# The last half row of a linear-kernel attention in two query parts, its last 256 tokens closed tile against tile

## The chip, the cores and the metric

The kernel runs on one core of one Trainium2 chip. The core has five engines that run side by side, each through its own list of instructions in order: TensorE (PE, matrix multiplication; PEld are its weight loads), VectorE (DVE), ScalarE (ACT), GpSimd (POOL) and SyncE (SP, which here only issues DMAs). They wait for one another through semaphores. The metric is the device time of one launch in microseconds; the median of several runs counts.

## What is computed

Four blocks follow one another on an input of 4 rows of 1024 tokens, 256 features each (4096 tokens). The third block is the one that the change touches, and the fourth begins where it ends:

```python
x = x + _layernorm(_L0_attn_ref(_layernorm(x), ...))      # gated attention
x = x + _layernorm(_L0_ffn_ref(_layernorm(x), ...))       # low-rank feed-forward
x = x + _layernorm(_L1_attn_ref(_layernorm(x), ...))      # the block of the change
x = x + _layernorm(_L1_ffn_ref(_layernorm(x), ...))       # experts, each with its 1024 best tokens

def _L1_attn_ref(x, w_qkv, w_out, b_out, gamma, beta):    # 16 heads of 16 features
    def kernel_func(q, k):
        scores = jnp.einsum('bhqd,bhkd->bhqk', q, k) / jnp.sqrt(HD)
        w = jax.nn.relu(scores)
        return w / (jnp.sum(w, axis=-1, keepdims=True) + KERN_EPS)
    ...
    out = jnp.einsum('bhqk,bhkd->bhqd', kernel_func(q, k), v)
    y = x + out @ w_out + b_out
    return layernorm(y) * gamma + beta

def _L1_ffn_ref(x, Wg, W1, b1, W2, b2):
    S = sigmoid(x @ Wg).T                                  # 8 experts x 4096 tokens
    G, I = jax.lax.top_k(S, 1024)
    ...
```

The weights of the attention are a plain `relu` of the scores; the sum that divides them comes out of the same matmul as the values, as a 17th column of ones.

## The kernel before

**Tiling of the attention.** Tokens come in tiles of 128; a half row is 512 tokens (`TB`, four tiles, `NJ = 4`), and there are eight half rows, `t` = 0 to 7. For the 512 queries of a half row the loop runs over four head groups `g` (four heads at a time) and within each over the eight key tiles `kt` of the row: 32 steps. `g` splits into `t, r = divmod(g, 2)`: two groups, `r` = 0 and 1, fill one half `t` of the 256 features.

**One step.** `scores` (L1225) gives four matmuls of 32 rows each, one head per 32-row strip of TensorE, side by side: 128 keys against 512 queries. Two of them go to single PSUM banks (tag `s`, three banks that the rest of the attention's small matmuls share), two to a pair of banks (tag `d`, two pairs). ScalarE applies `relu` to each single (L1242), VectorE to the pair in one instruction (L1243); the results stand in one of two `w` tiles. `weigh` (L1246) multiplies them with the values, four heads at a time on column strips, and adds over the key tiles into one bank, `po`. The weighing of a step stands behind the scores of the next one, so TensorE's order is scores(i+1), weighing(i).

**End of a head group.** `finish` transposes `po` on VectorE into `turned` (L1281). After `r` = 1 `divide` follows: `by_weight` adds a small constant, inverts and multiplies (L1110 to L1112), `back` transposes into `oT` (L1120).

**Closing a half row.** `close` makes the list of what follows the attention of a half row: `project_out` (eight matmuls `pt` per two tiles, L1135, and the sum `y`, L1142), then, tile by tile for each kind of step: statistics of `y` (`scale_of`: three VectorE instructions, then a power on GpSimd, L1064 to L1067), `affine` (two VectorE instructions, L1155 and L1156), statistics again, `shift` (a small VectorE instruction `msc`, L1160, then ScalarE adds it to `x`, L1162), `add` (L1167), statistics of `x`, and `token_rows` (the normalized token `hg`, L1178, and its DMA to `tok_d`, on SP's queue; after the last tile also `x` to `x_d`). Then `turn_gating` (four transposes per two tiles, `tpg`, L1193, and ScalarE's copy), and `gate` (`pg`, L1207, added to `logits`, L1215).

**The order around it.** The order on TensorE, VectorE and ScalarE is as the program writes it. Two lists hold what is still to do: `beside` (steps with TensorE work) and `rest` (the others). After each step of the attention `go_on` takes one entry of `beside` and one of `rest`, or two of `rest` if `beside` had one; at the last key tile of a group it takes none of `rest`. So the closing of one half row runs beside the attention of the next. The last half row has no next one: after the loop all that is left is emptied, with matmuls of no use (`keep_busy`, L206, which write to an `idle` bank) put in, 8 at first and 63 after the projections.

**After it.** The stage of the experts starts with the sigmoid of `logits` (L1361 to L1364), a search for each expert's threshold in 15 rounds (`ge`, L1394), and the gathering of tokens. SP also brings the experts' biases and weights (L1336 to L1345).

## Time and profile before

| | us |
|---|---|
| median of 3 runs (1630.09 to 1633.78) | 1633.39 |
| the profiled execution, its time | 1633.18 |
| its span | 1631.2 |
| TensorE busy in it | 1569.7 |
| VectorE busy | 920.7 |
| ScalarE busy | 634.7 |
| GpSimd busy | 403.3 |

The page also cuts the span into 40 equal slices of 40.8 us; a digit is the busy share in tenths, and PEclk is the clock granted to TensorE in tenths of full speed:

```profile
PE   7999999999999999999999999983999999999997
DVE  4555566664657787878787888878211211222145
ACT  3344444544544545454545454521121121211233
PEclk9999999999999999999999999995999999999999
```

The attention of the change is the stretch of 7s and 8s of VectorE. Its last half row ends in the slice with an 8 for TensorE; the 3 with half a clock behind it is the search for the thresholds.

In all times below, 0 is the start of the span unless another start is named. A line of the timeline or of the chain of waits gives the start, the length, the engine, the line of the kernel, what is written and read, the number of records, and in brackets the idle time ahead of it with what ended it. A matmul of 32-bit numbers leaves two records, one for each of its two passes.

### The profile page before, as it was taken

How to read it: one execution, taken by the hardware profiler on the slowest of the kernel's cores; microseconds unless marked ns; L12 is line 12 of the kernel's file. 1: busy time of each engine (PE TensorE's matmuls, PEld its weight loads, DVE VectorE, ACT ScalarE, POOL GpSimd, SP SyncE). 2: the span in 40 equal slices, each digit the busy share in tenths (PEclk: the TensorE clock that was granted, in tenths of full speed). 3: DMA queues.
4: the chain of work that ended last, by engine and by line, in shares of the span. 5: the costliest groups of instructions: out<-in, count | busy, mean ns of one | idle time of the engine just before them, and what ended most of it. 6: DMA issues, size and time to landing. Idle time of an engine off the chain costs nothing.

```text
span 1631.2 us, 22623 instructions
## 1 busy us (share of the span) xinstructions
PE 1569.7 (96%) x8787; PEld 778.2 (48%) x8787; DVE 920.7 (56%) x2085; ACT 634.7 (39%) x1101; POOL 403.3 (25%) x439
## 2 busy tenths in 40 slices
PE   7999999999999999999999999983999999999997
PEld 3666666666322232222323222231757667566674
DVE  4555566664657787878787888878211211222145
ACT  3344444544544545454545454521121121211233
POOL 4123232222201011111111001010423324324555
PEclk9999999999999999999999999995999999999999
DMA  8300000000000000101010100040133233234355
GB/s 205 120 1 1 1 1 1 0 1 1 1 1 1 23 18 7 34 7 34 1 40 1 39 2 27 14 168 4 53 78 69 66 74 72 66 75 89 65 148 136
DMA packets 70069, 71.15 MB, mean 44 GB/s; under 512 B 23597, under 2 KB 62922, under 8 KB 69834
## 3 DMA queue, kind: packets, MB, share of 16 engines
q1 hardware_dynamic: 56080, 47.01, 9.4%
q0 software_dynamic: 13008, 21.77, 7.4%
q8 instruction: 69, 1.13, 0.3%
q10 hardware_dynamic: 874, 0.93, 0.2%
q14 instruction: 38, 0.31, 0.1%
HBM read 41.74 MB, written 27.95 MB: 43 GB/s over the span
## 4 chain that ended last, share of the span: by engine, by line
PE 92%; DVE 4%; issue 1%; POOL 1%; ACT 1%; DMA 1%; POOLq 0%; SPq 0%; DVEq 0%; ACTq 0%
PE sc L1233 16%; PE po L1249 16%; PE ph L1712 13%; PE py L1735 13%; PE pg L691 4%; PE py L799 4%; PE pv L707 3%; PE ph L855 2%; PE po L771 2%; PE pt L1135 2%; PE pv L380 2%; PE pq L356 2%; PE pq L876 2%; PE po L775 2%; PE pk L356 2%; PE pkv L786 1%
## 5 line engine op out<-in xcount | busy, mean ns | idle before, releaser
L1243 DVE TENSOR_SCALAR w<-sc 128x1024 f32<-128x1024 f32 x256 | 312.7, 1222 | 97.4 <-PE sc L1233 65.1
L1242 ACT ACTIVATE w<-sc 128x512 f32<-128x512 f32 x512 | 278.0, 594 | 229.6 <-PE sc L1233 102.5
L1233 PE MATMUL sc<-qT,kT 32*128 32x512 f32 x2048 | 293.6, 639 | 1.4 <-ACT w L1242 0.8
L1249 PE MATMUL po<-w,vaug 128*17 128x512 f32 x2048 | 274.7, 598 | 1.3 <-DVE turned L1281 0.3
L1735 PE MATMUL py<-w,hid 128*128 128x256 f32 x1024 | 230.1, 380 | 0.0
L1719 ACT ACTIVATE hid<-ph,mb 128x512 f32<-128x512 f32 (+1 forms) x136 | 90.1, 662 | 344.4 <-PE ph L1712 343.3
L1712 PE MATMUL ph<-xT,w 128*128 128x512 f32 (+1 forms) x544 | 222.8, 567 | 0.7 <-DVE xT L1696 0.7
L1735 PEld LDWEIGHTS py<-w,hid 128*128 128x128 f32 x1024 | 191.1, 190 | 32.0 <-issue 7.0
L1233 PEld LDWEIGHTS sc<-qT,kT 32*128 32x128 f32 x2048 | 80.7, 183 | 184.9 <-issue 170.7
L1712 PEld LDWEIGHTS ph<-xT,w 128*128 128x128 f32 x544 | 103.2, 190 | 111.1 <-issue 107.6
L1249 PEld LDWEIGHTS po<-w,vaug 128*17 128x17 f32 x2048 | 35.3, 95 | 200.3 <-issue 171.0
L1754 POOL DMA_INDIRECT acc_d<-y,idx x56 | 88.1, 1573 | 157.0 <-issue 131.8
L1752 DVE TENSOR_TENSOR y<-py,mb 128x256 f32<-128x256 f32 x56 | 23.4, 418 | 142.3 <-PE py L1735 140.3
L1521 POOL DMA_INDIRECT got<-tok_d,idx x64 | 65.8, 1028 | 152.1 <-DVE idx L1511 135.0
L1696 DVE COPY xT<-tp 128x512 f32<-128x512 f32 (+1 forms) x34 | 22.3, 660 | 91.7 <-PE tp L1691 91.7
L1067 POOL TENSOR_TENSOR rsg<-veg,mhalf 128x1 f32<-128x1 f32 x32 | 17.7, 554 | 219.5 <-DVE veg L1066 219.5
L691 PE MATMUL pg<-nT,wh 128*128 128x512 f32 x128 | 61.4, 611 | 1.5 <-ACT nT L630 1.5
L799 PE MATMUL py<-wo,oT 128*128 128x256 f32 x256 | 61.9, 385 | 0.0
L707 PE MATMUL pv<-wh,nT 128*128 128x512 f32 x128 | 59.7, 592 | 0.0
L1511 DVE CAST idx<-parts 128x8 int32<-128x8 f32 x8 | 1.3, 167 | 101.8 <-PE parts L1509 101.8
L799 PEld LDWEIGHTS py<-wo,oT 128*128 128x128 f32 x256 | 47.3, 190 | 17.2 <-issue 9.4
L572 POOL TENSOR_TENSOR x<-x,y 128x1024 f32<-128x1024 f32 x14 | 32.9, 2351 | 73.3 <-ACT y L561 73.3
(277 smaller groups left out, 1927.5 us busy)
## 6 DMA issues: line engine op xcount, KB each, us to landing
w<-in_L_ffn_W_dram SPq DMA_DIRECT2D x16, 1024.0 KB, 5.7
x<-in_L_attn_x_dram SPq DMA_DIRECT2D x8, 512.0 KB, 5.0
acc_d<-logits SPq DMA_DIRECT2D x8, 512.0 KB, 4.2
x_d<-x SPq DMA_DIRECT2D x8, 512.0 KB, 3.0
tok_d<-hg SPq DMA_DIRECT2D x32, 128.0 KB, 1.7
back_w<-acc_d SPq DMA_DIRECT2D x6, 512.0 KB, 7.4
out_dram<-x SPq DMA_DIRECT2D x20, 128.0 KB, 1.7
out_dram<-back_w POOLq DMA_DIRECT2D x4, 512.0 KB
```

The lines of the kernel that those rows point to most:

```text
L691: nc.tensor.matmul(pg, lhsT=wh[:, c, HID + e * P : HID + (e + 1) * P], rhs=d["nT"][:, c, :], start=(c == 0), stop=(c == DC - 1),)
L707: nc.tensor.matmul(pv, lhsT=d["nT"][:, c, i * P : (i + 1) * P], rhs=wh[:, c, 0:HID], start=(c == 0), stop=(c == DC - 1),)
L799: nc.tensor.matmul(py, lhsT=d["oT"][:, e, :], rhs=wo[:, e, :], start=(e == 0), stop=(e == EC - 1))
L1233: nc.tensor.matmul(sc, lhsT=row["kT"][t][rows, r, kt * P : (kt + 1) * P], rhs=row["qT"][rows, t, qh * TB : (qh + 1) * TB], start=True, sto ...
L1242: nc.scalar.activation(w[:, j, :], sc, AF.Relu)
L1243: nc.vector.tensor_scalar(w[:, 2:4, :], pair, 0.0, None, ALU.max)
L1249: nc.tensor.matmul(po[32 * j : 32 * j + HD + 1, :], lhsT=row["v"][:, kt, HQ * t + 2 * j + r, :], rhs=w[:, j, :], start=(kt == 0), stop=(kt ...
L1521: return nc.gpsimd.indirect_dma_start(out=dst, out_offset=None, in_=rows[:, :], in_offset=self.at_chunk(c), bounds_check=NT - 1, oob_is_er ...
L1712: nc.tensor.matmul(ph, lhsT=w1[:, c, f * P : (f + 1) * P], rhs=xT[u][:, c, h * n : (h + 1) * n], start=(c == 0), stop=(c == DC - 1),)
L1719: nc.scalar.activation(hid[:, f, h * n : (h + 1) * n], ph, AF.Gelu, bias=mb1[:, e * FC + f : e * FC + f + 1])
L1735: nc.tensor.matmul(py, lhsT=hid[:, f, i * P : (i + 1) * P], rhs=w2[:, f, :], start=(f == 0), stop=(f == FC - 1),)
L1754: scatter = nc.gpsimd.indirect_dma_start(out=acc_d[:, :], out_offset=lists[e].at_chunk(k), in_=y, in_offset=None, bounds_check=NT - 1, oob ...
```

## The change

Only the last half row (`t` = 7) is treated differently in the attention, by `halves = 2`; everywhere else `halves` is 1 and the program is as before.

- Its 512 queries are taken in two parts of 256 (`q2` = 0, 1). A step takes two key tiles, so each part has 16 steps; a step has eight score matmuls of 256 columns, and eight weighing matmuls of 256 columns. Both key tiles of a head share a bank. `r` = 0 and 1 use separate halves of `po`.
- In every second step of this half row ScalarE applies `relu` to the pair of banks as well, in one instruction of 1024 columns.
- `go_on` takes two entries of `rest` per step there, four if `beside` had one, and the last key tile of a group is no exception.
- The first part's two tiles are closed through the lists, beside the second part. The second part's two are closed by a new function, `at_once`: each kind of step for one tile, then for the other, with the statistics of both and one power on GpSimd for the two (`moments`). Projection and gate are taken apart into halves; `shift` is not used there (the mean is subtracted from `y` on VectorE instead).
- The filling matmuls are 4 and 34 there, for 8 and 63. In the experts' stage 13 stand for 9.

```diff
+            def moments(tag, src, part):
+
+                st, mv, ve, rs = gating.setdefault(
+                    tag, [wk.tile([P, 2, w], F32, tag=f"{k}z", name=f"{k}{tag}") for k, w in zip(("st", "mv", "ve", "rs"), (6, 2, 1, 1))]
+                )
+                if part == "take":
+                    for k, i in enumerate(tiles):
+                        nc.vector.bn_stats(st[:, k, :], src[:, i, :])
+                    for k in range(2):
+                        nc.vector.bn_aggr(mv[:, k, :], st[:, k, :])
+                    nc.vector.tensor_scalar(ve[:, :, 0], mv[:, :, 1], EPS, None, ALU.add)
+                    nc.gpsimd.tensor_tensor(rs[:, :, 0], ve[:, :, 0], mhalf[:, 0:2], ALU.pow)
+                return [(i, mv[:, k, 0:1], rs[:, k, :]) for k, i in enumerate(tiles)]
+
+            def at_once(by_weight, back):
+
+
+                x, stt = xs[t], nc.vector.scalar_tensor_tensor
+                pts = [(i, side([P, D], "pt")) for i in tiles]
+                for i, pt in pts:
+                    project_tile(pt, i, (0,))
+                idle = ps.tile([P, 2, TB], F32, tag="d", name="idle", bufs=2)[:, 0, :]
+                keep_busy(idle, 4)
+                by_weight()
+                back()
+                for i, pt in pts:
+                    project_tile(pt, i, (1,))
+                keep_busy(idle, 34)
+                for i, pt in pts:
+                    nc.vector.tensor_tensor(y[:, i, :], pt, h[:, i, :], ALU.add)
+                scales = moments("b", y, "take")
+                for i, mean, rs in scales:
+                    stt(y[:, i, :], y[:, i, :], mean, gam, ALU.subtract, ALU.mult)
+                for i, mean, rs in scales:
+                    stt(y[:, i, :], y[:, i, :], rs, bet, ALU.mult, ALU.add)
+                scales = moments("c", y, "take")
+                for i, mean, rs in scales:
+                    nc.vector.tensor_scalar(y[:, i, :], y[:, i, :], mean, None, ALU.subtract)
+                for i, mean, rs in scales:
+                    stt(x[:, i, :], y[:, i, :], rs, x[:, i, :], ALU.mult, ALU.add)
+                for i, mean, rs in moments("g", x, "take"):
+                    token_rows(i, mean, rs)
+                turn_gating(tiles[0])
+                gate()
...
-            for j, sc in enumerate((*singles, pair[:, 0, :], pair[:, 1, :])):
-                rows = slice(32 * j, 32 * (j + 1))
-                nc.tensor.matmul(
-                    sc,
-                    lhsT=row["kT"][t][rows, r, kt * P : (kt + 1) * P],
-                    rhs=row["qT"][rows, t, qh * TB : (qh + 1) * TB],
-                    start=True,
-                    stop=True,
-                )
+            for m in range(halves):
+                for j, sc in enumerate((*singles, pair[:, 0, :], pair[:, 1, :])):
+                    rows = slice(32 * j, 32 * (j + 1))
+                    nc.tensor.matmul(
+                        sc[:, m * n : (m + 1) * n],
+                        lhsT=row["kT"][t][rows, r, (kt + m) * P : (kt + m + 1) * P],
+                        rhs=row["qT"][rows, t, q0 : q0 + n],
+                        start=True,
+                        stop=True,
+                    )
 
             for j, sc in enumerate(singles):
                 nc.scalar.activation(w[:, j, :], sc, AF.Relu)
-            nc.vector.tensor_scalar(w[:, 2:4, :], pair, 0.0, None, ALU.max)
+            if halves > 1 and kt // halves % 2:
+
+                nc.scalar.activation(w[:, 2:4, :], pair, AF.Relu)
+            else:
+                nc.vector.tensor_scalar(w[:, 2:4, :], pair, 0.0, None, ALU.max)
             return w
 
+        def weighed(halves, r):
+
+            return slice(0, TB) if halves == 1 else slice(r * TB // 2, (r + 1) * TB // 2)
...
-                for g in range(NG):
-                    for kt in range(KT):
-                        w = scores(row, qh, g, kt)
-                        if before is not None:
-                            finish(*before)
-
-                        go_on(0 if kt == KT - 1 else 1)
-                        before = (row, b, qh, g, kt, w)
+                halves = 2 if (b, qh) == (B - 1, BPB - 1) else 1
+                for q2 in range(halves):
+                    for g in range(NG):
+                        for kt in range(0, KT, halves):
+                            w = scores(row, qh, q2, halves, g, kt)
+                            if before is not None:
+                                finish(*before)
+
+                            at_end = kt == KT - halves
+                            go_on(halves if halves > 1 or not at_end else 0)
+                            before = (row, b, qh, q2, halves, g, kt, w)
             row = after
         finish(*before)
-        idle = ps.tile([P, 2, TB], F32, tag="d", name="idle", bufs=2)[:, 0, :]
-        keep_busy(idle, 8)
-        while rest and not beside:
-            go_on()
-        while beside:
-            go_on()
-
-        keep_busy(idle, 63)
         while beside or rest:
             go_on()
+        state["close"][0](*divide(state, DC - 1))
...
-            keep_busy(idle, 9)
+            keep_busy(idle, 13)
```

`weigh`, `finish`, `divide`, `close`, `token_rows`, `turn_gating` and `gate` get the same arguments (`halves`, the part's tiles, its columns) and work on them.

## The prediction

> **What bounds the kernel now.** I read the page's costliest groups first, then the windows, then the chain of waits around the end of the attention, then the timeline of the last half row.

> ```profile
> L1243 DVE TENSOR_SCALAR w<-sc 128x1024 f32<-128x1024 f32 x256 | 312.7, 1222 | 97.4 <-PE sc L1233 65.1
> L1242 ACT ACTIVATE w<-sc 128x512 f32<-128x512 f32 x512 | 278.0, 594 | 229.6 <-PE sc L1233 102.5
> L1233 PE MATMUL sc<-qT,kT 32*128 32x512 f32 x2048 | 293.6, 639 | 1.4 <-ACT w L1242 0.8
> L1249 PE MATMUL po<-w,vaug 128*17 128x512 f32 x2048 | 274.7, 598 | 1.3 <-DVE turned L1281 0.3
> ```

> TensorE bounds the attention: its score and weighing groups were idle 1.4 and 1.3 us in 256 steps. A step is 1.07 us of scores and 0.98 us of weighing (starts in the timeline: 1041.04, 1042.12, 1043.10), so 2.05 us. The last half row is 32 steps; its first score starts at 993.82, its last weighing is over at 1069.41, where the filling matmuls start: 75.6 us.

> ```profile
> 993.82:1069.55 75.73, 75.16 (x554) 19.23 (x554) 60.78 (x104) 39.92 (x73) 6.60 (x12) 1.00 0.04 15
> 1069.55:1096.28 26.73, 24.32 (x115) 12.13 (x114) 20.34 (x67) 3.47 (x7) 6.86 (x12) 1.00 0.70 239
> 1100.00:1110.00 10.00, 0.98 (x6) 0.41 (x4) 8.72 (x48) 5.36 (x4) 0.00 (x0) 0.55 0.21 13
> ```

> Columns: length, then busy time of PE, PEld, DVE, ACT, POOL, then granted clock. In the first row VectorE has 15 us to spare in 75.7, ScalarE 36. In the second the 24.3 us of TensorE are filling matmuls; the path is VectorE:

> ```profile
> 1068.50 1.03 PE po L1249 x8
> 1069.55 0.73 DVE turned L1281
> ...
> 1072.40 3.30 PE pt L1135 x14
> 1075.73 0.69 DVE y L1142
> ...
> 1079.52 0.68 POOL rsb L1067
> 1080.21 0.48 DVE y L1156
> ...
> 1086.75 0.56 POOL rsc L1067
> 1087.49 1.58 DVE x L1167 x4
> ...
> 1092.09 0.43 DVE hg L1178
> 1092.65 1.43 PE tpg L1193 x8
> ...
> 1095.84 0.44 DVE logits L1215
> ```

> From 1069.41 to the logits' end at 1096.28 are 26.9 us for four tiles of 128 tokens, with nothing beside them. The change trades this tail against the half row before it.

> **The tail, now two tiles.** Counted from the end of the last weighing; next to each step its row. A VectorE operation that needs the one before starts 0.035 us after it, another 0.08 us before its end. Halved widths go by the sums: 0.69 us for 512 columns (L1142), 0.42 for 256 (L800), so the transposes of 0.70 become 0.44 and the division's 0.69 becomes 0.42. Start +0.14; turned 0.44, den 0.17, reciprocal 0.25, even 0.42, oT 0.44 end at 2.0. The first halves of both projections and 4 fillers (0.97 + 0.9) lie under that. Second halves: one projection matmul is 0.48 (eight records 1.93), the first sum starts at 2.6, the second ends at 3.5. Statistics of two tiles: 2 x 0.42 + 2 x 0.18 + 0.15 with starts, end at 4.7. POOL's power (0.55 to 0.69) hides under two subtract-and-scale of 0.47; the second pair ends at 6.4. Statistics again to 7.6; the power hides under two subtractions of 0.35; adding ends at 9.1. Statistics to 10.3; here the power is bare: 11.0. Two hg of 0.40 end at 11.8, four transposes to 12.4, ScalarE's copy 0.59 to 13.0, half a gate (0.97 / 2) to 13.6, logits 0.42: 14.1. So 26.9 becomes 14.1: **-12.8 us**.

> **What the half row pays.** Moved into it are one projection (1.93), one turning of two tiles (0.60), half a gate (0.48) of its own first part, and the gate of the half row before (0.97), which lay in the tail under VectorE and now comes earlier because twice as many steps of the queue are popped per step: +4.0 us of TensorE in line.

> Matmuls are 256 columns wide, twice as many, each with its own weights. The nearest row has row tiles of 256 columns:

> ```profile
> 210.92 1.13 PE L895 MATMUL py<-v,qT 64*128 64x256 f32 x8
> 211.98 0.70 PE L691 MATMUL pg<-nT,wh 128*128 128x512 f32 x1
> ```

> Four passes of 256 columns on each of two tiles, 1.06 us, as long as two passes of 512 in the scores (1.07): only the first load shows. The gate (four column-tiled passes, eight records) has 0.97, as the weighing's 0.98. So I take 0; bounds 0 and +0.21 us per step (two further loads at the 0.11 us that lie between the first and second load of a score group) = 0 to +6.7.

> [...] L895 shows second loads on the same row group hidden; I go by the row. [...]

> Every second step ScalarE takes all weights: 0.59 each for the singles, which start 0.50 apart, then 1024 columns. No such row; 256 columns cost 0.47 and 512 0.69 in L1719, so 512 more add 0.43: 1.02 (bounds: 0.9, and 1.2 as two calls). ScalarE starts 0.14 after the scores (1042.12, 1042.26 in the timeline), and TensorE 0.05 after a weight is there (VectorE's ended at 1040.02, the load below starts at 1040.07): the last weight is there 0.15 + 2.0 + 0.06 = 2.2 us after the scores; the weighing wants it after 0.98 + 1.07 = 2.05. So 0.16 of wait in eight of the 16 steps, where no inline work covers it: 1.3. The last step has no scores to cover it: 2.2 - 0.98 = 1.2. Sum +2.5 (bounds 1.3 to 4.3).

> **The backlog**, the largest term. The queue of closing work now gives 2 pieces per step, 4 where a TensorE piece goes with them, instead of 1 and 2, while the work of the half row before stays four tiles. I followed VectorE's program order (0 = first score): w0, turned, division, oT end at 5.0; the projection 5.1 to 7.0; then sum 0.69, two hg, two statistics (0.74 each: 1007.28 to 1008.02) to 9.9; w2 to 11.2. Before w4 now stand a sum, two statistics, four affine pairs (0.99 each: 1013.12 to 1014.11) and two statistics: 7.6, so w4 runs 18.8 to 20.0. The scores of step 5 were over at 17.8: **2.3 us of wait**. ScalarE has a second one: its shifts (L1162) stand ahead of step 5's singles and wait for msc, which comes after two more statistics at 22.1; two shifts to 23.2, so the first bank of step 5 is free at 23.8, where step 6's scores stood since 21.1: **2.8 us**, then 0.7 of echoes and 0.2 at the first projection. In the second part the same shape, two tiles: w18 ends at 59.5, wanted at 57.0: **2.5 us**, 0.3 after it. Together 8.8, plus 0.8 at the opening, in both kernels. Such waits exist already, small:

> ```profile
> 1040.07 0.12 PEld L1249 LDWEIGHTS po<-w,vaug 128*17 128x17 f32 x4 [0.31 <-DVE w L1243]
> 1041.85 0.51 ACT L1162 ACTIVATE x<-x,msc 128x256 f32<-128x256 f32 x1 [0.98 <-DVE msc L1160]
> ```

> Sum: 32 x 1.07 + 33 x 0.985 (one weighing is left over from before) = 66.7; inline 3 x 1.93 + 4 x 0.60 + 2.5 x 0.97 = 10.6; waits 0.8 + 8.8 + 2.5 = 12.1: 89.4 us. The same counting of the kernel before gives 75.1 where the trace has 75.6, so 89.4 to 89.9: **+14 us**. Bounds: backlog 3 to 12.

> **The rest.** 13 fillers for 9 at L1366: 2.8 us at the 0.215 of the tail's fillers, ahead of transposes that want a reciprocal ending 3.3 us after the logits: 0 (+2.3 if the clock is halved there). 34 fillers end at 10.3 of 11.8: no cost, and the clock stays. SP now issues the first expert's loads ahead of the last tok_d rows; the first use of expert weights is at 1148, the gather past 1141, 45 us behind the logits: 0. Removing the wait of a weighing for the transposition (the two r use separate halves of po): -0.3 over the whole page, inside the count.

> Net -12.8 + 14 = +1.2 on the profiled run's 1633.2 (span 1631.2, 2 us around it; the median is 1633.4): **1635 us**, own range 1631 to 1639. A measurement here can tell 0.3% (4.9 us) from no change, so this forecast is "no change", leaning slow. Chance 0.57.

> **Rivals.** (1) *The backlog hides.* For it: VectorE's 15 us to spare, and ScalarE takes 16 x 1.22 from it. Against: the order puts 7.6 us between two weights. Then waits are 3.3 + the inline 4.0 - 12.8 + noise: about -6.5, 1627. Chance 0.14. (2) *Second loads stand bare* in the 256-column scores: +6.7 on the forecast, 1641.5, slower. Decides from 0.12 us per step. For it: four row tiles, twice L895's two; against: L895, L1207. Chance 0.10. (3) *The waits grow*: TensorE stands 2.3 and 2.8 us within 5 us, and the trace's clock was 0.55 where it was mostly idle (1100 to 1110). Half clock for two steps costs 4, and longer ScalarE calls (1.2) 1.8: 1640. Decides from a stall a third longer. Chance 0.19.

> **Numbers.** Faster: rival 1 less its edge, 0.13. Slower: rivals 2 and 3, whose centres lie past 1638.3, with little of the forecast: 0.29. Same 0.58. Range 1628 to 1641: it leaves out half of rival 1 and of rivals 2 and 3's upper parts.

> **What would show it.** Right: last weighing some 90 us after the half row's first score, logits' end 14 us later; two waits of 2 to 3 us near 20 and 24 us and one near 59; score groups of eight at 1.07. Wrong: groups at 1.2 or more (rival 2), clock under 1.00 before the logits (3), no wait over 1 us between 15 and 30 us (1), or a tail above 15.5.

## The result, and the profile after

| | before | after |
|---|---|---|
| median, us | 1632.55 (1630.09 to 1633.78, 20 runs) | 1635.5 (1634.68 to 1637.35, 20 runs) |
| ratio, 95% interval | | 1.0022 (1.0015 to 1.0029) |
| span of the profiled execution | 1631.2 | 1633.1 |
| first score of the last half row | 993.82 | 993.53 |
| last half row, to the end of its last weighing | 75.59 | 90.55 |
| tail, to the end of the logits | 26.85 | 14.90 |
| the rest, to the end of the span | 534.98 | 534.12 |

The change makes the kernel 0.22% slower: less than the 0.3% that was called no change, though the interval leaves out zero. The tail gave 11.95 us and the half row took 14.96; the start and the rest gave back 1.15. That is 1.9 us more in the two profiles; the medians lie 2.95 apart, since the profile before is 0.6 above its median and the one after 0.5 below. The end of the half row is taken in all kernels 0.1 us before the end of its last record, where the next work on TensorE starts.

These are the costliest groups of the attention on the page after; they answer to those of before:

```profile
L1306 DVE TENSOR_SCALAR w<-sc 128x1024 f32<-128x1024 f32 x240 | 293.1, 1222 | 112.3 <-PE sc L1292 72.8
L1292 PE MATMUL sc<-qT,kT 32*128 32x512 f32 (+1 forms) x2304 | 296.5, 589 | 2.9 <-ACT w L1301 2.3
L1318 PE MATMUL po<-w,vaug 128*17 128x512 f32 (+1 forms) x2304 | 276.5, 552 | 5.5 <-DVE turned L1351 2.7
```

VectorE has 16 weights less (240 for 256). TensorE's idle time ahead of scores and weighings rose from 2.7 us on the whole page to 8.4; 6.3 of these lie in the last half row (its two groups are shown at e1). The means of the two TensorE groups now mix two shapes and say nothing.

The stretches, in the columns of before's table; the second lies inside the first:

```profile
993.53:1084.10 90.57, 84.32 (x1093) 46.09 (x1092) 54.77 (x132) 55.74 (x93) 10.20 (x18) 0.96 0.07 22
1014.90:1021.70 6.80, 5.33 (x37) 2.39 (x40) 3.32 (x12) 4.55 (x9) 1.10 (x2) 0.50 0.01 2
1084.10:1098.98 14.88, 12.30 (x56) 5.98 (x55) 9.94 (x33) 0.58 (x1) 2.30 (x3) 1.00 0.48 176
```

VectorE is busy for 54.8 of 90.6 us, so by the average it has more room than before (60.8 of 75.7), and yet TensorE waits for it: the queue's order decides, not the sum. The granted clock is no longer 1.00 in the half row: for 6.8 us it was 0.50.

The timeline there, with the wait ahead of a group in brackets:

```profile
1012.08 1.23 DVE L1306 TENSOR_SCALAR w<-sc 128x1024 f32<-128x1024 f32 x1
1013.71 1.06 PE L1318 MATMUL po<-w,vaug 128*17 128x256 f32 x16 [2.67 <-DVE turned L1351]
...
1015.82 0.91 ACT L1162 ACTIVATE x<-x,msc 128x256 f32<-128x256 f32 x2 [6.55 <-DVE msc L1160]
1017.26 2.08 PE L1292 MATMUL sc<-qT,kT 32*128 32x256 f32 x14 [1.47 <-ACT w L1301]
1019.27 1.91 PE L1318 MATMUL po<-w,vaug 128*17 128x256 f32 x16
1021.11 1.41 PE L1292 MATMUL sc<-qT,kT 32*128 32x256 f32 x16
1022.45 1.06 PE L1318 MATMUL po<-w,vaug 128*17 128x256 f32 x16
```

The two waits that the prediction placed at 20 and 24 us after the first score end at 20.2 and 23.7 (1013.71 and 1017.26 less 993.53). The first stands behind VectorE's late weight (w, 1012.08 to 1013.31) and then for `turned`, the transposition of the head group before, which VectorE has behind that weight: it ends at 1013.66, the weighing starts at 1013.71. The second stands behind ScalarE, idle for 6.55 us until `msc` came. The second is 1.47 us by its bracket and 2.4 by the pitches, since two of the sixteen score records (1.08 us at half clock) run ahead of it. Behind it fourteen score records and the weighing take 2.08 and 1.91 us, where whole groups of sixteen elsewhere take 1.15 and 1.06: that is the halved clock (0.50 from 1014.9 to 1021.7).

The rest of the half row, from the timeline of TensorE (the next group's start less a group's own is its pitch; its length also holds the overlap with the next):

```profile
1048.53 1.15 PE L1292 MATMUL sc<-qT,kT 32*128 32x256 f32 x16
1049.61 1.06 PE L1318 MATMUL po<-w,vaug 128*17 128x256 f32 x16
1050.60 1.15 PE L1292 MATMUL sc<-qT,kT 32*128 32x256 f32 x16
...
1054.09 1.04 PE L1318 MATMUL po<-w,vaug 128*17 128x256 f32 x12 [1.80 <-DVE w L1306]
...
1066.14 1.03 PE L1213 MATMUL pg<-hTg,wgp 128*32 128x256 f32 x4
1067.10 1.15 PE L1292 MATMUL sc<-qT,kT 32*128 32x256 f32 x16
...
1074.49 1.18 PE L1318 MATMUL po<-w,vaug 128*17 128x256 f32 x16
1075.60 1.15 PE L1292 MATMUL sc<-qT,kT 32*128 32x256 f32 x16
```

Eight scores of 256 columns have a pitch of 1.08 us, and the weighing 0.99, as four of 512 had (1.07 and 0.98 in before). The third wait is 1.80, near 60 us. Half a gate (four records) takes the place of 0.96 us, no less than the whole one of eight records (1008.94 to 1009.90, also 0.96). The weighing behind a step of ScalarE's has 1.11 instead of 0.99 (1074.49 to 1075.60).

The tail, from the chain of waits (start, length, what):

```profile
1084.23 0.46 DVE turned L1351
...
1088.91 0.88 POOL rsb L1235
...
1091.86 0.74 POOL rsc L1235
...
1094.73 0.70 POOL rsg L1235
...
1096.02 0.79 PE tpg L1198 x4
...
1097.47 1.06 PE pg L1213 x4
...
1098.56 0.44 DVE logits L1222
```

The same kinds of work as in before's chain, for half the tiles and tile against tile; what the prediction had most too small is `pg`.

### The profile page after: what moved, and what is told of

Its sections match the earlier page's. It is cut to its first block, busy times and chain, and to the rows that moved or that the text cites. A ratio compares the mean times of both kernels' runs of the same rounds, so it can differ in the third digit from the quotient of the medians.

```text
span 1633.1 us, 23586 instructions
## 1 busy us (share of the span) xinstructions
PE 1567.2 (96%) x9270; PEld 800.4 (49%) x9270; DVE 904.5 (55%) x2080; ACT 647.4 (40%) x1115; POOL 401.3 (25%) x436
## 4 chain that ended last, share of the span: by engine, by line
PE 91%; DVE 5%; issue 2%; ACT 1%; POOL 1%; DMA 0%; POOLq 0%; ACTq 0%; DVEq 0%
PE sc L1292 16%; PE po L1318 15%; PE ph L1781 13%; PE py L1804 13%; PE py L799 4%; PE pg L691 4%; PE pv L707 3%; PE ph L855 2%; PE po L771 2%; PE pv L380 2%; PE pt L1134 2%; PE pq L356 2%; PE pq L876 2%; PE po L775 2%; PE pk L356 2%
## 5 line engine op out<-in xcount | busy, mean ns | idle before, releaser
L1306 DVE TENSOR_SCALAR w<-sc 128x1024 f32<-128x1024 f32 x240 | 293.1, 1222 | 112.3 <-PE sc L1292 72.8
L1292 PE MATMUL sc<-qT,kT 32*128 32x512 f32 (+1 forms) x2304 | 296.5, 589 | 2.9 <-ACT w L1301 2.3
L1318 PE MATMUL po<-w,vaug 128*17 128x512 f32 (+1 forms) x2304 | 276.5, 552 | 5.5 <-DVE turned L1351 2.7
L1292 PEld LDWEIGHTS sc<-qT,kT 32*128 32x128 f32 x2304 | 95.3, 185 | 176.3 <-issue 158.7
L1318 PEld LDWEIGHTS po<-w,vaug 128*17 128x17 f32 x2304 | 44.7, 96 | 196.9 <-issue 158.3
L1765 DVE COPY xT<-tp 128x512 f32<-128x512 f32 (+1 forms) x34 | 22.2, 659 | 90.6 <-PE tp L1760 88.1
L1067 POOL TENSOR_TENSOR rsg<-veg,mhalf 128x1 f32<-128x1 f32 x30 | 16.6, 554 | 202.7 <-DVE veg L1066 202.7
L691 PE MATMUL pg<-nT,wh 128*128 128x512 f32 x128 | 60.9, 608 | 1.5 <-ACT nT L630 1.5
```

The costliest lines, as they stand in the source:

```text
L691: nc.tensor.matmul(pg, lhsT=wh[:, c, HID + e * P : HID + (e + 1) * P], rhs=d["nT"][:, c, :], start=(c == 0), stop=(c == DC - 1),)
L1292: nc.tensor.matmul(sc[:, m * n : (m + 1) * n], lhsT=row["kT"][t][rows, r, (kt + m) * P : (kt + m + 1) * P], rhs=row["qT"][rows, t, q0 : q0 ...
L1306: nc.vector.tensor_scalar(w[:, 2:4, :], pair, 0.0, None, ALU.max)
L1318: nc.tensor.matmul(po[32 * j : 32 * j + HD + 1, weighed(halves, r)], lhsT=row["v"][:, kt + m, HQ * t + 2 * j + r, :], rhs=w[:, j, m * n : ...
```

## The experiments

All times of this section are medians; the ratio is against the kernel before, run on the same chip (there 1632.69, 1632.27 and 1632.92 us in the three sets: e1 to e4, e5 to e8, e9 to e11). The parts are read from one profile each:

| | half row | tail | rest | median | ratio (95%) |
|---|---|---|---|---|---|
| before | 75.59 | 26.85 | 534.98 | 1632.55 | |
| after | 90.55 | 14.90 | 534.12 | 1635.5 | 1.0022 (1.0015 to 1.0029) |
| e1, queue as before | 82.64 | 15.77 | 534.28 | 1627.71 | 0.9969 (0.9957 to 0.9981) |
| e2, shift on VectorE | 87.38 | 14.91 | 534.31 | 1631.06 | 0.9992 (0.9983 to 1.0002) |
| e3, VectorE takes all pairs | 93.70 | 14.91 | 534.27 | 1637.98 | 1.0031 (1.0020 to 1.0042) |
| e4, old closing | 90.54 | 16.81 | 532.50 | 1635.77 | 1.0021 (1.0012 to 1.0030) |
| e5, e1 and e2 | 82.34 | 15.63 | 534.38 | 1626.86 | 0.9966 (0.9954 to 0.9978) |
| e6, e1 and 40 fillers | 82.62 | 14.90 | 533.34 | 1627.01 | 0.9970 (0.9957 to 0.9982) |
| e7, all four edits | 81.68 | 14.91 | 534.30 | 1625.62 | 0.9961 (0.9948 to 0.9975) |
| e8, closing order alone | 75.59 | 25.67 | 534.57 | 1630.83 | 0.9990 (0.9981 to 0.9999) |
| e9, e7 with VectorE's pairs | 86.68 | 14.91 | 534.32 | 1631.15 | 0.9991 (0.9982 to 1.0000) |
| e10, e7 with a wait of 2 us | 83.79 | 14.91 | 534.10 | 1628.51 | 0.9976 (0.9967 to 0.9985) |
| e11, e7 with a wait of 5 us | 89.23 | 14.91 | 533.15 | 1632.77 | 1.0001 (0.9992 to 1.0010) |

### e1: the queue gives as many pieces per step as before

```diff
-        def go_on(room=1):
+        def go_on(room=1, twice=2):
...
-                room *= 2
+                room *= twice
...
-                            go_on(halves if halves > 1 or not at_end else 0)
+                            go_on(halves if halves > 1 or not at_end else 0, 2 // halves)
```

`beside` no longer doubles the room in the last half row: two entries of `rest` per step of two key tiles, not four.

> The changed kernel, but in the two-part half row the queue of closing work gives two pieces per step also where a TensorE piece goes with them (not four). Theory (the crowding of VectorE's list between two of its weights is what costs): VectorE reaches w4 about when the scores are there; the waits near 17, 21 and 57 us of the half row shrink from 2 to 3 us each to under 1, the clock stays at 1.00 in the half row, the half row takes 83 instead of 90.6 us, and the kernel 1628 to 1629, faster than before (1632.6) and than the change (1635.5). Rival (the split itself costs: half-wide matmuls, or ScalarE's long call in every second step): the half row stays above 88 us and the kernel above 1633.

The half row fell by 7.9 us and the median by 7.8. The two groups over the whole half row, e1's:

```profile
L1292 PE MATMUL sc<-qT,kT 32*128 32x256 f32 x512 | 37.7, 400 | 0.0
L1318 PE MATMUL po<-w,vaug 128*17 128x256 f32 x512 | 36.1, 382 | 1.4 <-DVE turned L1351 1.1 <-ACT w L1304 0.3
```

and the same of after:

```profile
L1292 PE MATMUL sc<-qT,kT 32*128 32x256 f32 x512 | 39.9, 411 | 1.5 <-ACT w L1301 1.5
L1318 PE MATMUL po<-w,vaug 128*17 128x256 f32 x512 | 37.0, 390 | 4.8 <-DVE turned L1351 2.7 <-DVE w L1306 1.8 <-ACT w L1304 0.3
```

The waits went from 6.3 us to 1.4, and the groups themselves became 3.1 us shorter (73.8 for 76.9), most of it since the clock stayed at 1.00. The work is the same, 512 records each: what cost the time was how many pieces stood between two weights. In e1 the clock fell instead near the end of the tail, from 1088.9 for 6.8 us (the logits end at 1091.4), so its tail is 15.77.

### e2: the shift on VectorE

```diff
         def shift(i, mean, rs):
+            if t >= B * BPB - 2:
+                nc.vector.tensor_scalar(y[:, i, :], y[:, i, :], mean, None, ALU.subtract)
+                return (rs,)
...
```

> The changed kernel, but the closings that run beside the two-part half row subtract the mean on VectorE (0.35 us a tile) in place of msc and ScalarE's shift. Theory (two waits in a row: VectorE's list, then ScalarE's list behind msc): the second wait of the opening goes, the first (2.5 us before the weighing of step 4) stays; -3.5 us on the half row, 1631 to 1632.5; if the first wait alone still halves the clock, 1 us of that is lost. Rival (VectorE's list is all that counts, and ScalarE's wait lies within it): within 0.5 us of the change, 1635 to 1636.

The wait behind ScalarE (1.47) is gone and the half clock lasts one stretch of 3.4 us, not two; the first wait stays, at 2.66. Half row -3.2, median -4.4 against after (its profiled execution, at 1632.55, is 1.5 above its median). So the second wait of the prediction had the cause it named: ScalarE's own queue held its weights.

### e3: VectorE takes every pair

```diff
-            if halves > 1 and kt // halves % 2:
+            if False:
```

> The changed kernel with VectorE taking the pair in every step, as elsewhere. Theory (ScalarE's part pays about for itself): it frees 16 x 1.22 us of VectorE and costs 0.15 us in some steps and 1.2 at the end; without it VectorE's list is worse, +1 us, 1636 to 1637.5. Rival (ScalarE's latency is what makes the change slow): faster than the change by 1 us or more, under 1634.5.

Half row +3.2, median +2.5, more than was expected: ScalarE's share is a gain, in spite of the later weights in every second step. A part of the 3.2 is the clock: it was 0.50 for three stretches here (1015.2 to 1025.4), for two in after. e9 has the comparison at full clock.

### e4: the closing order of before for the last two tiles

```diff
-                at_end = state["at_end"] = q2 == 1
+                at_end = state["at_end"] = False
...
+        idle = ps.tile([P, 2, TB], F32, tag="d", name="idle", bufs=2)[:, 0, :]
+        keep_busy(idle, 8)
+        while rest and not beside:
+            go_on()
+        while beside:
+            go_on()
+
+        keep_busy(idle, 44)
         while beside or rest:
             go_on()
-        state["close"][0](*divide(state, DC - 1))
```

> The changed kernel, but the second part's two tiles are closed through the lists, as the first part's are, with 8 and 44 filling matmuls. Theory (most of the 12 us gained in the tail come from two tiles in place of four; the alternating order hides two of three powers and a shift): the tail is 16.7 instead of 14.9 us, 1637 to 1638. Rival (the order is what gains): the tail is 19 us or more, above 1639.

The tail is 16.81 as expected, 1.9 longer than with the new order, but the median rose by 0.3 only. In the profile the rest is 1.6 us shorter, all of it ahead of the first expert matmul (50.8 us behind the logits in e4, 52.4 in after), and it arises at two runs of fillers. The 13 behind the search take 4.33 us in e4 and 5.29 in after, as the half clock of the search ends 36.8 and 38.8 us behind the logits: there e4 gains 1.0. A later run of 15 takes 3.40 and 4.99, as after has a second dip of the clock (1144.6 to 1148.0) and e4 none: there it gains the other 0.6. So the gain of the order was there at the logits and was given back later. Whether every execution gives it back was not tried.

### e5, e6 and e7: the edits together

e5 is e1 with e2. e6 is e1 with 40 fillers in `at_once`:

```diff
-                keep_busy(idle, 34)
+                keep_busy(idle, 40)
```

e7 has all of these, and the very last pair back on VectorE, since nothing covers ScalarE's lateness there:

```diff
-            if halves > 1 and kt // halves % 2:
+            if halves > 1 and kt // halves % 2 and (g, kt, q2) != (NG - 1, KT - 2, 1):
```

> Two pieces per step throughout (as in e1_queue_single) and the mean subtracted on VectorE (as in e2_shift_on_vector). Theory (both act on the same two waits, so the second has little left to take): the half row 82 instead of 82.6 us, 1626.5 to 1627.7. Rival (ScalarE's wait behind msc is a loss of its own): 3.5 us less than e1_queue_single, as e2_shift_on_vector had 4.5 less than the change: 1624 to 1625.

> e1_queue_single with 40 filling matmuls in the tail in place of 34. In its profile the tail was 15.8 us with the clock at 0.50 from 13 us after the last weighing; in the change's 14.9 at 1.00. Theory (34 fillers end 1.5 us before the transposes want TensorE, and whether the clock falls there depends on where the execution meets a fixed grid of time): with 40 the tail is 14.9 and the clock 1.00; the median within 1 us of e1_queue_single, 1626.7 to 1627.7, with less spread. Rival (the fillers hold up the transposes): the tail longer than 15.5 at full clock.

> e1_queue_single, the subtraction on VectorE, 40 fillers, and VectorE taking the pair in the very last step, where ScalarE's three calls had 1.2 us with no scores to cover them. Theory: the wait at the end falls from 1.2 to 0.3 us; half row 81, tail 14.9, 1625 to 1626.5. Rival (the clock's grid hides differences of 1 us): equal to e5_single_and_shift within 0.3 us.

With the queue uncrowded the shift is worth 0.3 us of half row, not 3.2: its wait was a consequence of the crowd. In e6's profile the six fillers take the tail back from 15.77 to 14.90 with the clock at 1.00; by the medians this is 0.7 us, and the two ratios' intervals overlap. e7's half row is 81.68, 0.66 below e5. Its median is the lowest, though its interval overlaps those of e1, e5 and e6: 6.4 us (0.39%) under the kernel before (1632.55 x 0.0039), and, by the two ratios, 0.6% under the changed one.

### e8: the closing order alone

The half row as before, with four tiles closed by `at_once` (66 fillers):

```diff
-                keep_busy(idle, 34)
+                keep_busy(idle, 66)
...
-                halves = 2 if (b, qh) == (B - 1, BPB - 1) else 1
+                halves = 1
```

> The kernel before with the alternating order of closing alone: all 512 queries in one part, ScalarE takes no pair, and the four tiles of the last half row are closed step by step in turn, with one power on GpSimd for four, 4 and 66 fillers. Theory (the order hides powers and the shift, and costs the half row nothing): half row 75.6, tail 23.5 in place of 26.9, 1629 to 1630. Rival (the tail is bound by VectorE's sum of work, which the order leaves alone): 26 us or more, 1632 to 1633.

The tail is 25.67, only 1.2 below before, where 23.5 was expected. With the 1.9 of e4 this says that most of the 12 us that the change takes from the tail comes from closing half as many tiles there and not from the order. The chain of e8 shows three places where the order's gain may have gone:

```profile
1072.56 1.92 PE pt L1134 x8
1075.35 1.73 PE pt L1134 x8
...
1077.07 14.24 PE idle L206 x66
...
1091.32 0.45 PE tpg L1198 x4
...
1092.43 1.55 PE pg L1213 x8
```

The projections begin late, since a turning and a gate of the half row before still stand ahead of them (from 1069.96, after 1.14 us of wait for their tokens, to 1072.5). Four fillers (0.86) stand in the chain between the two halves of the projections. And the 66 fillers end only at 1091.31, where the first two tiles of tokens were there some half a microsecond before. No run took one of these out, so how much each costs is not shown.

### e9: what ScalarE's share is worth in the uncrowded queue

e7, with `if False:` for its condition on ScalarE.

> The version with all four edits (1625.6 us), but VectorE applies relu to the pair of banks in every step of the last half row; ScalarE takes none. Theory: ScalarE's share is worth about as much here as in the changed kernel with its crowded queue, because VectorE has the closing of a half row beside it in either case: 16 calls of 1.22 come back to VectorE, some 20 us, of which about 15 find room. By the program order the last half row then lasts 86 to 87.5 us against 81.7, time 1630 to 1631.5. Rival: ScalarE's share is only needed where the queue is crowded (there it was worth 2.3 us in the median); with the uncrowded queue VectorE keeps up: half row within 1 us of 81.7, time 1625 to 1626.5.

Half row +5.0 and median +5.5 (4.9 by the two ratios), with the clock at 1.00 in both half rows: the share is worth more here than in the crowded queue (3.2). TensorE's timeline in e9:

```profile
1012.88 0.61 PE L1321 MATMUL po<-w,vaug 128*17 128x256 f32 x4
1014.43 1.04 PE L1321 MATMUL po<-w,vaug 128*17 128x256 f32 x12 [0.94 <-DVE w L1309]
...
1016.48 0.61 PE L1321 MATMUL po<-w,vaug 128*17 128x256 f32 x4
1017.61 1.04 PE L1321 MATMUL po<-w,vaug 128*17 128x256 f32 x12 [0.52 <-DVE w L1309]
...
1019.66 1.62 PE L1321 MATMUL po<-w,vaug 128*17 128x256 f32 x16
```

A weighing begins on ScalarE's two weights, four records alone, and stands for VectorE's pair; the other twelve then take 1.04 us, where all sixteen together take 1.06. So a late pair costs its wait and, by an estimate from these lengths, some 0.6 us for the four records ahead of it (0.61), and of the last of these groups (1.62 for 1.06) the brackets show nothing. In e7, with ScalarE's share, no bracket in the half row names a weight of VectorE's.

### e10 and e11: the price of a wait

e7, with VectorE writing one pair's weights three or five times (the same values), in one step of the second part:

```diff
-                nc.vector.tensor_scalar(w[:, 2:4, :], pair, 0.0, None, ALU.max)
+                for _ in range(3 if (halves, q2, g, kt) == (2, 1, 2, 0) else 1):
+                    nc.vector.tensor_scalar(w[:, 2:4, :], pair, 0.0, None, ALU.max)
```

> The version with all four edits, and VectorE writes the weights of one pair three times instead of once, in one step in the middle of the second part (the same values: nothing else differs). So a known lateness of 2 x 1.22 us is put on VectorE at one place where TensorE is otherwise fed. VectorE's weight is some 0.6 us early there, so the weighing should wait 1.9 us. Theory of the short wait: it costs just that, clock 1.00 throughout the half row, half row 83.5, time 1627.5. Rival (any wait near 2 us brings the clock down, as the one of 2.67 did in the changed kernel): a stretch of 3.4 us at half clock follows, cost 1.9 + 1.7, half row 85.3, time 1629.2.

> As before, but the weights of that pair are written five times: 4 x 1.22 us late, a wait of 4.3 us. Theory (a wait over about 2.7 us brings the clock down for one or two stretches of 3.4 us): cost 4.3 + 1.7 to 3.4, half row 87.7 to 89.4, time 1631.6 to 1633.3. Rival (the clock does not follow the wait; it fell in the changed kernel for another reason): cost 4.3, clock 1.00, half row 86.0, time 1629.9.

The timeline of e10, then of e11:

```profile
1060.84 1.06 PE L1322 MATMUL po<-w,vaug 128*17 128x256 f32 x16 [2.16 <-DVE turned L1355]
```

```profile
1063.60 1.91 PE L1322 MATMUL po<-w,vaug 128*17 128x256 f32 x16 [4.67 <-DVE turned L1355]
1065.43 2.09 PE L1295 MATMUL sc<-qT,kT 32*128 32x256 f32 x16
1067.46 1.91 PE L1322 MATMUL po<-w,vaug 128*17 128x256 f32 x16
1069.30 0.94 PE L1201 MATMUL tpg<-ident,hg 128*128 128x128 f32 x4
1070.17 1.15 PE L1295 MATMUL sc<-qT,kT 32*128 32x256 f32 x16
```

In e10 a wait of 2.16 us cost 2.1 in the half row, nothing besides. In e11 a wait of 4.67 cost 7.55: the clock was 0.50 from 1063.1 to 1069.9, and the groups behind the wait have nearly twice their length (1.91 for 1.06, 2.09 for 1.15). The extra 2.9 us (7.55 less 4.67) is the second price of a wait.

## Why the prediction was right, and where its sum was off

The total: 1635 was forecast and 1635.5 measured, with the mechanism that was named: a tail 12 us shorter, paid for by work and waits in the half row, with the three long waits where it placed them. That the total is only 0.5 off is partly luck. The sum, 1633.2 + 1.2, is 1634.4 and not 1635, and it starts from a profiled execution 0.6 above the median of the 20 runs; and the rest gave back 0.9 that the sum does not have. Against the profile the net is +1.9 us where the sum had +1.2; term by term:

- **The tail**, 14.1 predicted, 14.90 measured. Half a gate was taken as 0.97 / 2. It is not half: its four records took 1.06 in the tail, where the eight of a whole gate take 1.03 in the half row (at 1008.94). That is 0.57 of the 0.8 us. VectorE's halved operations (0.44, 0.18, 0.25, 0.42) came out as the sums had them. GpSimd's powers did not hide: for two tiles they took 0.88 and 0.74 us, for 0.55 to 0.69, and VectorE waited 0.20 and 0.33 us for the first two. Smaller differences elsewhere gave some 0.3 back.
- **Inline work**: the same half gate took 0.96 instead of 0.48 in the half row; projections 2.00, 1.93 and 1.92 against 1.93. So the half-gate term, +0.48 twice, should have been two whole gates: it is a term mis-sized by a wrong reading.
- **Second weight loads**, taken as 0 by L895: score groups have a pitch of 1.08, weighings 0.99, for 1.07 and 0.98 in before. Rival 2, to be decided from 0.12 us per step, falls.
- **ScalarE's odd steps**: 0.12 per step (1.11 less 0.99) for 0.16. The call of 1024 columns took 1.03 for 1.02. The last step's 1.2 is there: the weighing before starts at 1080.93, so the last would end at 1082.98 (0.99 and 1.06 later) and ends at 1084.20. Giving that pair back to VectorE brought 0.66 (e7 against e5, whose other difference lies in the tail).
- **The backlog**, 8.8 predicted: the first wait cost 2.73 for 2.3 (from 1009.90, the start of the scores ahead of it, to 1013.71, less 1.08). The 0.4 is the transposition. The sum had taken the wait of a weighing for it as removed, since the two `r` use separate halves of `po`; it is not, and e7's only waits in the half row are two of that kind, 1.1 us. The second, with its echoes, cost 4.6 for 3.5 (scores at 1023.44, where undisturbed pitches from 1013.71 would have them at 1018.8): by an estimate from the pitches 2.4 of wait, for 2.8, and 2.2 of halved clock (1.07, 0.85 and 0.26 in the groups of 2.08, 1.91 and 1.41 us), where the sum had 0.7 of echoes. The third cost 2.7 for 2.8 (2.40 by 1055.06 and 0.29 behind it). Some 10.1 in all. e1 and e2 show the causes: with fewer pieces 7.9 us go, with the shift elsewhere the second wait goes. The halved clock is what the backlog's sum left out; the forecast had put it into rival 3 alone.
- **Rival 3** came true in small. Its point of decision, a stall a third longer than forecast, was not reached, and the clock fell all the same; but 1.47 of the 6.8 us at half clock were the second wait, in which TensorE stood anyway, and its 1640 did not come. The prediction's list would have called a clock under 1.00 this rival: the list was too coarse.
- **Rival 1** (the backlog hides, 1627) is what e1 makes of the change: 1627.71. Its sum as written, 3.3 + 4.0 - 12.8, is -5.5 and not -6.5; without the 0.8 of the opening, which both kernels have, it is -6.3. Its chance hung on the order of the queue, which the program fixes.
- **The rest**, taken as 0, gave 0.86. It is not the search: the half clock there lasts one stretch of 3.4 us less (1107.0 to 1137.8 after, 1101.0 to 1135.1 before), but from the logits' end to the first expert matmul both kernels take 52.4 us. It lies behind the last expert matmul, which starts 11.8 us before the end of the span in before and 10.9 in after. e1 and e6 have 10.9 there too, and e7 12.1, so it does not follow the change; its cause stays open.

## What to carry to other kernels

When work is moved beside a loop, count what stands between two instructions that the bounding engine waits for, in the order written; VectorE's 15 us to spare in the average did not keep two weights from being over 2 us late, and spreading the same pieces out was worth 7.8 us. Price a wait by its length and by the clock behind it (2.16 us cost 2.1 in e10, 4.67 cost 7.55 in e11 with the clock at 0.50), and half an operation not by half its time: the half gate took 0.96 us, as the whole one did. If a moved step leaves its engine for another, ask what stands ahead of it there: the shift waited on ScalarE with the next weights behind it.

## What was not expected of the hardware

| kernel, start of the stretch | share covered | clock in the next stretch |
|---|---|---|
| e11, 1059.7 | 0.00 | 0.50 |
| e4, 1011.4 | 0.33 | 0.50 |
| after, 1011.5 | 0.34 | 0.50 |
| e5, 1085.7 | 0.39 | 0.50 |
| e2, 1012.3 | 0.41 | 0.50 |
| e3, 1011.7 | 0.43 | 0.50 |
| e1, 1085.4 | 0.44 | 0.50 |
| e2, 1049.8 | 0.47 | 1.00 |
| e4, 1052.3 | 0.50 | 1.00 |
| e8, 1096.3 | 0.50 | 0.50 |
| after, 1052.4 | 0.51 | 1.00 |
| e3, 1056.1 | 0.53 | 1.00 |
| e10, 1059.2 | 0.53 | 1.00 |

In these rows a clock of 0.50 followed every share up to 0.44, and one of the six shares from 0.47 to 0.53. Behind a stretch at half clock the next was again at 0.50 where the share was 0.57 (after), 0.80 (e1), 0.85 (e11) and 0.88 and 0.86 (e3), and at 1.00 behind 1.00 (after) and 0.85 (e5). After's wait of 2.67 us lies in a stretch with 0.34, and 0.50 followed; its wait of 1.80 lies in one with 0.51, and 1.00 followed. That the price of a wait depends on where the stretches begin is an inference from these rows; no run chose their offset.

The share alone does not sort all of them. Behind the search, between 1133 and 1149, seven of the profiles (before, after, e2, e3, e5, e9, e10) have a stretch covered to 0.71 to 0.74 with half clock behind it, after's dip at 1144.6 among them (0.71; 0.72 in before), while shares of 0.54 to 0.68 elsewhere (0.59 and 0.65 in after's tail, 0.67 in before's) kept full clock. What sets these apart is not shown.

The clock fell to 0.50 at the waits of 2.34 us in e3, 2.66 in e2 and 2.67 in after; at the wait of 2.16 in e10 it stayed at 1.00.

**Fillers have an end as well as a beginning.** The tail of e1 in TensorE's timeline:

```profile
1078.67 7.50 PE L206 MATMUL idle<-same_b 128*128 128x512 bf16 x34
1087.56 0.78 PE L1198 MATMUL tpg<-ident,hg 128*128 128x128 f32 x4 [1.39 <-DVE hg L1178]
1089.02 1.91 PE L1213 MATMUL pg<-hTg,wgp 128*32 128x256 f32 x4 [0.67 <-ACT hTg L1201]
```

The 34 fillers end at 1086.17, 1.39 us before the transposes, and with what follows the stretch from 1085.4 is covered to 0.44; the clock was 0.50 from 1088.9, and the half gate took 1.91 us, for 1.06. Six more fillers (e6) kept every stretch of the tail at 0.75 or more and the clock at 1.00. After's own tail has the same 34 and the same 1.39; its stretches lay so that the lowest shares were 0.59 and 0.65, and the clock stayed.
